# Order of one ScalarE copy and two exponentials in a multi-query attention kernel

## The chip, the cores and the metric

The kernel runs on one core of a Trainium2 chip. The metric is the device time of one execution in microseconds (us); smaller is better. The engines that matter here are TensorE (PE in the profile, with PEld for its weight loads), VectorE (DVE), ScalarE (ACT), GpSimd (POOL) and the DMA queue of SyncE (SP). Each engine executes its own list of instructions in the order in which the program wrote them and waits for others by semaphores.

## The reference

Residual multi-query attention over 64 sequences of 128 tokens with 512 features, 16 heads of 64 and one shared key and value head:

```python
xn = layernorm(x, g_in)
q = (xn @ Wq).reshape(b, n, H, DH).transpose(0, 2, 1, 3) * scale
kv = xn @ Wkv                      # k, v, with one null key and value put ahead
...
sim = jnp.einsum('bhid,bjd->bhij', q, k) + bias
sim = jnp.where(causal_mask, neg, sim)
sim = jnp.where(mask_p[:, None, None, :], sim, neg)
attn = jax.nn.softmax(sim, axis=-1)
out = jnp.einsum('bhij,bjd->bhid', attn, v)
out = out.transpose(0, 2, 1, 3).reshape(b, n, INNER) @ Wo
return x + layernorm(out, g_out)
```

All data is 32-bit floating point.

## The kernel before

The 64 sequences are worked in 32 pairs. After a first part that fills the pipeline, a loop calls `turn(d)` and `body(d)` for d = 1 to 29; three pairs at the end have code of their own. Everything is written out by hand in program order, under a manual schedule: the order of the calls in `body` is the order on each engine, and the framework only puts in the semaphore waits.

One `body(d)` holds the work of several pairs at once. With a = 2d and b = 2d+1 it computes the softmax of sequences a and b; with p = 2d-2 the output projection of the pair before; with l = 2d-4 the output layer norm, residual and store of the pair before that; and, for the group of four sequences g = d//2 + 1, half of its query projection. The parity h = d % 2 says which half: `f0` is the first tile of 128 query features in this call, `f1` the second. In bodies with h = 0 GpSimd also prepares sums of tokens (`token_sum`, `token_sums_inner`).

The query projection multiplies 2 by 2 blocks with seven products in place of eight (the Strassen-Winograd scheme). `product(g, f, k, pool, tag)` (matmul at L539) computes product k as two matrix instructions, which the profile shows as four matmul passes of 256 columns, into a PSUM bank with the tag "a" or "c". Bank "a" collects products 1, 6, 7 and 4 of a tile, one on top of the other. After each of the first three, `keep` (L551) has ScalarE copy the running sum out of the bank to SBUF (`kp` after product 1, `ku` after 6 and 7), and the next product into that bank must wait for this copy, since it adds to what is being read. Bank "c" collects products 5 and 3. `q_out` adds a kept copy to a bank on VectorE (L560) or, for the last one, copies it on ScalarE (L557). Product 2 is itself replaced by seven smaller ones (`inner_product`, L605, tile `pl`), and the output projection is built in the same way (`out_product`, L892; its first bank "X" is copied by ScalarE at L906 to `kyp`).

`exps(b, hf, lo, hi)` (L707) computes the exponentials of heads lo to hi-1 of one half of the rows: one ACTIVATE per head, each followed by a short read of its accumulator. Then `rinv` (L725, VectorE) and `scale` (L729, GpSimd) divide by the sums. `pair_norm` (L950, ScalarE, `yn`) and `norm_apply` (L301, ScalarE) are normalisations; `norm_stats` ends in a power on GpSimd at L280.

The stretch of `body` around the change, for TensorE: product 1 of tile f0, one or two inner products, the eight passes of `out_product(p, 1)`, then products 6, 5 and 7 of f0, then `out_product(p, 2)` (`pyw`). For ScalarE: the copy `kp`, `pair_norm(l)`, four exponentials of b, the copy `kyp`, two exponentials of b (heads 4 and 5), the copy `ku` of product 6, `pair_norm(l + 1)`, two more exponentials (heads 6 and 7), the copy `ku` of product 7, two `norm_apply`, one exponential of a, and the copy `qT` of bank "a" after product 4. Body 1 differs a little: there is no pair l yet, so that ScalarE has no `pair_norm` there, and a whole product 2 stands in place of the inner ones.

Of the kernel before, what the change touches and what calls it, by code (L numbers as in the profile page):

```python
# [17 lines left out]
def kernel(  # L18
# [504 lines left out]
    def product(g, f, k, pool, tag, start=True):  # L523

        if start:
            prod[tag] = pool.tile([P, HT], FP, tag=tag, name=f"p{tag}_{g}_{f}_{k}")
        lo, hi = xT[g][:, 0 : GB // 2], xT[g][:, GB // 2 :]
        t1, t2, t3, t4 = (xS.get((g, i)) for i in range(1, 5))
        w, t = {
            1: (a11, lo[:, :, lo_k]),  # L530
            2: (a12, lo[:, :, hi_k]),
            3: (s4, hi[:, :, hi_k]),
            4: (a22, t4),
            5: (s1, t1),
            6: (s2, t2),
            7: (s3, t3),
        }[k]
        for kc in range(HK):
            nc.tensor.matmul(  # L539
                prod[tag],  # L540
                w[:, kc, f * P : (f + 1) * P],
                t[:, :, kc, :],
                start=(start and kc == 0),
                stop=(kc == HK - 1),
                skip_group_check=not start,
            )

    def keep(tag, name, slot=None):
        slot = slot or name
        kept[name] = bp.tile([P, HT], FP, tag=f"k{slot}", name=f"k{name}", bufs=1)  # L550
        nc.scalar.copy(kept[name], prod[tag])  # L551
# [150 lines left out]
    def exps(b, hf, lo=0, hi=R8):  # L702
        if hf == 0 and lo == 0:
            rsum[b] = small.tile([P, 2, R8], FP, tag="rsum", name=f"rsum_{b}")
        for k in range(lo, hi):
            row = S[b][:, k, WITH_NULL[hf]]
            nc.scalar.activation(  # L707
                row,
                row,
                AF.Exp,  # L710
                bias=nmax[b][:, hf, k : k + 1],
                accum_out=rsum[b][:, hf, k : k + 1],
            )
# [146 lines left out]
    def out_sum(p, k, eng=nc.gpsimd):  # L860

        h11, h12 = oT[p][:, 0], oT[p][:, 1]
        h21, h22 = oT[p + 1][:, 0], oT[p + 1][:, 1]
        if k == 0:
            yS[p] = bp.tile([P, HC, N], FP, tag="yS", name=f"yS_{p}", bufs=1)
        o, a, b, op = (
            (yS[p], h21, h22, ALU.add),
            (h11, yS[p], h11, ALU.subtract),
            (h21, h22, h11, ALU.subtract),
            (h12, h12, h11, ALU.subtract),  # L870
        )[k]
        eng.tensor_tensor(o, a, b, op)  # L872
# [73 lines left out]
    def pair_norm(b, odd=(None, None)):  # L946
        nmr, rstd = nmrs.pop(b)
        pool, tag = odd if b % 2 else (ps_s, "s")
        yn[b] = pool.tile([P, DIM], FP, tag=tag, name=f"yn_{b}")
        nc.scalar.activation(yn[b], ys[b], AF.Identity, bias=nmr, scale=rstd)  # L950
# [318 lines left out]
    def body(d):  # L1269

        a, b, p, l = 2 * d, 2 * d + 1, 2 * d - 2, 2 * d - 4
        g, h = d // 2 + 1, d % 2
        q, soft = g < NG, d > 0
# [62 lines left out]
        if out:  # L1336
# [1 line left out]
            out_keep("X", "yp1", "yp1")  # L1338
            out_sum(p, 1)
            out_sum(p, 2)  # L1340
        if soft:
            exps(b, 0, 4, 6)
        if q:
            product(g, f0, 6, ps_q, "a", start=False)
            keep("a", "u2")
        if ln:
            pair_norm(l + 1, (ps_y, "Y"))
        if q:
# [253 lines left out]
    for d in range(1, PAIRS - 2):  # L1602
        turn(d)
        body(d)
# [42 lines left out]
```

## Time and profile before

| | |
|---|---|
| median of 3 runs | 1039.6 us (1039.45 to 1039.65) |
| the profiled execution, its own time | 1039.67 us |
| span of that execution in the trace | 1037.9 us |
| TensorE matmul busy | 1024.5 us, 99% |
| TensorE weight loads busy | 903.0 us, 87% |
| VectorE, ScalarE, GpSimd busy | 76%, 65%, 72% |
| from product 6 of one body to that of the second after it, in the middle of the run | 63.34 us (482.12 to 545.46), so 31.67 us a body with its turn |

The span is what the trace covers; the time of the execution is 1.8 us longer. A row of a timeline holds the start in us from the span's start, the length in us, the engine, the source line, the operation, the output and inputs, the shapes, how many instructions were merged ("x4"), and in brackets the idle time of the engine just before, with what ended it. A merged row's length runs from the first start to the last end. Matmuls are pipelined: the next starts before the last has ended, so rows of one engine overlap, and a matmul's end is modelled, while its start is recorded.

### The profile page before, as it was taken

Reading aid. Unit: us, or ns where it says so; the run is one execution under the profiler, and the core shown is the slowest. Engines: PE = TensorE matmul, PEld = TensorE weight load, DVE = VectorE, ACT = ScalarE, POOL = GpSimd, SP = SyncE. Lnnn points to the kernel's source line nnn. Section 1 sums busy time; section 2 is a strip of 40 time slices with the busy share of each in tenths; the row PEclk is TensorE's granted clock in tenths of the full one; section 3 lists DMA queues with packets and bytes.
Section 4 is the critical chain, followed back from the end, with each engine's and each line's share of the span. In section 5 each row is a group of like instructions: output and inputs, shape, how many; then the busy total and the mean of one; then the engine's idle time right before and its main releaser. Section 6 shows DMA issues by size and latency. Waiting matters only on the chain.

```text
span 1037.9 us, 31399 instructions
## 1 busy us (share of the span) xinstructions
PE 1024.5 (99%) x12337; PEld 903.0 (87%) x12337; DVE 788.7 (76%) x1774; ACT 675.7 (65%) x2709; POOL 745.1 (72%) x579
## 2 busy tenths in 40 slices
PE   9999999999999999999999999999999999999997
PEld 8888888888888888888888888888888888888886
DVE  6867777877778877778777778777787777877697
ACT  4756667666577565676656776666766657856582
POOL 4997668686785857758677686766868678586676
PEclk9999999999999999999999999999999999999999
DMA  6514152231613315133151521415223151331211
GB/s 215 167 40 135 63 171 77 77 112 63 182 66 103 99 60 176 63 123 108 41 166 62 158 85 47 148 62 172 76 83 110 62 183 62 104 82 33 93 63 63
DMA packets 69228, 105.14 MB, mean 101 GB/s; under 512 B 9044, under 2 KB 33496, under 8 KB 67288
## 3 DMA queue, kind: packets, MB, share of 16 engines
q1 hardware_dynamic: 68784, 102.73, 31.7%
q8 instruction: 97, 1.59, 0.6%
q14 instruction: 51, 0.42, 0.1%
q10 hardware_dynamic: 296, 0.40, 0.1%
HBM read 67.45 MB, written 35.65 MB: 99 GB/s over the span
## 4 chain that ended last, share of the span: by engine, by line
PE 85%; ACT 6%; DVE 6%; issue 1%; POOL 1%; DMA 0%; POOLq 0%; DVEq 0%; ACTq 0%
PE pa L539 17%; PE pyX L892 15%; PE pyY L892 10%; PE pc L539 7%; PE po L805 7%; PE pkv L353 6%; PE pyw L892 5%; PE pl L605 4%; ACT s L707 3%; PE ps L676 3%; PE pq L474 3%; PE sc_X L676 2%; DVE st L269 2%; DVE nmax L698 2%; PE sc_Y L676 2%; PE py_s L892 1%
## 5 line engine op out<-in xcount | busy, mean ns | idle before, releaser
L707 ACT ACTIVATE s<-s,nmax 128x65 f32<-128x65 f32 (+1 forms) x1024 | 372.7, 368 | 62.5 <-DVE nmax L698 62.5
L729 POOL TENSOR_TENSOR s<-s,rinv 128x512 f32<-128x512 f32 (+1 forms) x132 | 190.7, 1447 | 166.3 <-DVE rinv L725 166.3
L641 POOL TENSOR_TENSOR s<-biasp,mneg 128x1552 f32<-128x1552 f32 (+1 forms) x65 | 205.9, 3170 | 51.2 <-DVE s L691 38.2
L707 ACT ACTIVATION_READ_ACCUMULATOR s<-s,nmax 128x1 f32 x1024 | 195.6, 191 | 0.0
L557 ACT COPY qT<-pa 128x256 f32<-128x256 f32 x59 | 22.0, 373 | 172.0 <-PE pa L539 172.0
L539 PE MATMUL pa<-xS,wq 128*128 128x256 f32 x472 | 123.7, 385 | 3.6 <-ACT ku L551 2.6
L698 DVE TENSOR_REDUCE nmax<-s 128x8 f32<-128x1032 f32 (+1 forms) x128 | 121.7, 951 | 0.1
L745 DVE STREAM_TRANSPOSE sb<-s 128x1536 f32<-128x1536 f32 (+1 forms) x68 | 113.6, 1673 | 2.0 <-POOL s L729 2.0
L892 PE MATMUL pyX<-wo,oT 128*128 128x256 f32 x464 | 109.7, 379 | 0.0
L892 PE MATMUL pyX<-wT,oT 128*128 128x256 f32 x464 | 109.7, 379 | 0.0
L539 PEld LDWEIGHTS pa<-xS,wq 128*128 128x128 f32 x472 | 85.1, 190 | 23.9 <-POOL rstd L280 7.0
L892 PEld LDWEIGHTS pyX<-wo,oT 128*128 128x128 f32 x464 | 86.0, 190 | 10.5
L892 PEld LDWEIGHTS pyX<-wT,oT 128*128 128x128 f32 x464 | 85.9, 190 | 10.7
L872 POOL TENSOR_TENSOR oT<-oT 128x512 f32<-128x512 f32 x64 | 80.5, 1277 | 4.3 <-PE pyw L892 2.0
L560 DVE TENSOR_TENSOR qT<-pc,ku 128x256 f32<-128x256 f32 x118 | 48.7, 413 | 45.9 <-PE pc L539 29.7
L805 PE MATMUL po<-sb,vr 32*64 32x128 f32 (+1 forms) x3840 | 81.5, 310 | 0.0
L805 PEld LDWEIGHTS po<-sb,vr 32*64 32x64 f32 x3840 | 71.3, 131 | 8.1 <-issue 5.7
L621 DVE TENSOR_TENSOR qT<-pl,kp 128x128 f32<-128x128 f32 x112 | 31.3, 279 | 57.9 <-PE pl L605 55.7
L824 ACT ACTIVATE oT<-po,nv 128x512 f32<-128x512 f32 (+1 forms) x127 | 73.8, 654 | 0.1
L280 POOL TENSOR_TENSOR rstd<-rstd,nhalf 128x1 f32<-128x1 f32 x64 | 35.2, 559 | 46.6 <-DVE rstd L279 44.2
L353 PE MATMUL pkv<-wkv,xT 128*128 128x128 f32 x512 | 65.2, 281 | 0.0
L353 PEld LDWEIGHTS pkv<-wkv,xT 128*128 128x128 f32 x512 | 59.6, 191 | 5.0 <-DVE s L691 4.8
(185 smaller groups left out, 2379.0 us busy)
## 6 DMA issues: line engine op xcount, KB each, us to landing
res<-in_x_dram SPq DMA_DIRECT2D x64, 256.0 KB, 2.9
x<-in_x_dram SPq DMA_DIRECT2D x63, 256.0 KB, 4.5
out_dram<-y SPq DMA_DIRECT2D x63, 256.0 KB, 2.0
xd<-xb SPq DMA_DIRECT2D x14, 1024.0 KB
xT<-xd SPq DMA_DIRECT2D x56, 256.0 KB, 6.0
vr<-vd SPq DMA_DIRECT2D x64, 128.0 KB, 2.7
kT<-kd SPq DMA_DIRECT2D x64, 64.0 KB, 2.1
wo<-in_L_cond_Wo_dram SPq DMA_DIRECT2D x1, 2048.0 KB, 13.4
```

The source lines that it names most:

```text
L353: nc.tensor.matmul(pkv, xT[g][:, t, kc, :], wkv[:, kc, :], start=(kc == 0), stop=(kc == KC - 1),)
L539: nc.tensor.matmul(prod[tag], w[:, kc, f * P : (f + 1) * P], t[:, :, kc, :], start=(start and kc == 0), stop=(kc == HK - 1), skip_group_ch ...
L641: nc.gpsimd.tensor_tensor(S[b][:, :, keys], biasp[:, :, keys], mneg[:, t, keys] .unsqueeze(1) .broadcast_to([P, R8, keys.stop - keys.start ...
L676: nc.tensor.matmul(home[r][u * DH : (u + 1) * DH, f, :], qT[g, f, t // 2][rows, t % 2, hf, u], kT[g][rows, 0 : nk // Q, t, :], start=True, ...
L698: nc.vector.tensor_reduce(nmax[b][:, hf], S[b][:, :, WITH_NULL[hf]], AX.X, ALU.max, negate=True)
L707: nc.scalar.activation(row, row, AF.Exp, bias=nmax[b][:, hf, k : k + 1], accum_out=rsum[b][:, hf, k : k + 1],)
L729: nc.gpsimd.tensor_tensor(sv, sv, rinvs[b, hf][:, lo:hi].unsqueeze(2).broadcast_to([P, hi - lo, sv.shape[2]]), ALU.mult,)
L745: nc.vector.transpose(sbs[b][:, :, lo:hi].rearrange("p j e q -> p e j q"), S[b][:, lo:hi, 1 : ROW - 1].rearrange("p e (j k) -> p e j k", k=Q),
L805: nc.tensor.matmul(po[s][rows, to : to + n], vr[g][quad, j, t, :], sb[quad, slots, r * NF : (r + 1) * NF, :], start=(turn == 0), stop=True ...
L824: nc.scalar.activation(to, src, AF.Identity, bias=nv2)
L872: eng.tensor_tensor(o, a, b, op)
L892: nc.tensor.matmul(prod[key], h[:, c, :], w[:, c, :], start=(start and c == 0), stop=(c == HC - 1), skip_group_check=not start,)
```

## The change

The call of `exps(b, 0, 4, 6)` moves behind product 6 and its `keep`. On ScalarE the copy of bank "a" after product 6 then stands ahead of the exponentials of heads 4 and 5, not behind them. It happens once in each of the 29 bodies. The order on TensorE, VectorE, GpSimd and the DMA queue is the same as before; nothing is added or left out.

```diff
         if out:
             out_product(p, 1, ps_y, "X")
             out_keep("X", "yp1", "yp1")
             out_sum(p, 1)
             out_sum(p, 2)
-        if soft:
-            exps(b, 0, 4, 6)
         if q:
             product(g, f0, 6, ps_q, "a", start=False)
             keep("a", "u2")
+        if soft:
+            exps(b, 0, 4, 6)
         if ln:
             pair_norm(l + 1, (ps_y, "Y"))
         if q:
             product(g, f0, 5, ps_q, "c")
         if soft:
             exps(b, 0, 6)
             rinv(b, 0)
         if q:
             product(g, f0, 7, ps_q, "a", start=False)
             keep("a", "u3")
```

## The prediction

> **What bounds the kernel now.** I read the page first: busy shares, then the chain that ended last.
>
> ```profile
> span 1037.9 us, 31399 instructions
> ...
> PE 1024.5 (99%) x12337; PEld 903.0 (87%) x12337; DVE 788.7 (76%) x1774; ACT 675.7 (65%) x2709; POOL 745.1 (72%) x579
> ...
> PE 85%; ACT 6%; DVE 6%; issue 1%; POOL 1%; DMA 0%; POOLq 0%; DVEq 0%; ACTq 0%
> ```
>
> TensorE is busy for 99% and carries 85% of the chain. No other engine is above 76%. So only time in which TensorE stands still, or runs slower than its own pitch, can be won. Yet 6% of the chain runs through ScalarE, so somewhere TensorE waits for it. The groups by line say where:
>
> ```profile
> L539 PE MATMUL pa<-xS,wq 128*128 128x256 f32 x472 | 123.7, 385 | 3.6 <-ACT ku L551 2.6
> L539 PEld LDWEIGHTS pa<-xS,wq 128*128 128x128 f32 x472 | 85.1, 190 | 23.9 <-POOL rstd L280 7.0 <-ACT ku L551 6.9 <-POOL yS L872 0.5
> ```
>
> The matmuls into bank "a" with a weight from wq idled 3.6 us in all, 2.6 of them for a copy `ku`. Their weight loads idled longer: 6.9 us for `ku` and 7.5 for something on GpSimd. Next I read TensorE's timeline in one body with h = 0 (from 482) and one with h = 1 (from 514):
>
> ```profile
> 482.12 1.03 PE L539 MATMUL pa<-xS,wS 128*128 128x256 f32 x4
> 482.98 1.03 PE L539 MATMUL pc<-xS,wS 128*128 128x256 f32 x4
> 484.17 1.10 PE L539 MATMUL pa<-xS,wq 128*128 128x256 f32 x4 [0.17 <-ACT ku L551]
> 485.11 1.89 PE L892 MATMUL pyw<-wo,oT 128*128 128x256 f32 x8
> ...
> 487.50 1.03 PE L539 MATMUL pa<-xS,wq 128*128 128x256 f32 x4
> ...
> 514.68 1.03 PE L539 MATMUL pc<-xS,wS 128*128 128x256 f32 x4
> 515.78 1.13 PE L539 MATMUL pa<-xS,wq 128*128 128x256 f32 x4
> 516.75 1.89 PE L892 MATMUL pyw<-wo,oT 128*128 128x256 f32 x8
> ```
>
> These are products 6, 5 and 7, then `pyw`. A product takes 0.86 (482.12 to 482.98). Product 7 should start 0.86 after product 5, at 483.84; it starts at 484.17. The starts of the weight loads show the same:
>
> ```profile
> 482.76 0.84 PEld L539 LDWEIGHTS pc<-xS,wS 128*128 128x128 f32 x4
> 484.14 0.73 PEld L539 LDWEIGHTS pa<-xS,wq 128*128 128x128 f32 x4 [0.54 <-POOL rstd L280]
> ...
> 515.78 0.73 PEld L539 LDWEIGHTS pa<-xS,wq 128*128 128x128 f32 x4 [0.47 <-ACT ku L551]
> ```
>
> And ScalarE over the same body:
>
> ```profile
> 482.74 0.36 ACT L906 COPY kyp<-pyX 128x256 f32<-128x256 f32 x1
> 482.99 0.36 ACT L707 ACTIVATE s<-s,nmax 128x65 f32<-128x65 f32 x1
> ...
> 483.33 0.35 ACT L707 ACTIVATE s<-s,nmax 128x65 f32<-128x65 f32 x1
> ...
> 483.67 0.36 ACT L551 COPY ku<-pa 128x256 f32<-128x256 f32 x1
> 483.92 0.79 ACT L950 ACTIVATE yn<-y,nmro,rstdo 128x512 f32<-128x512 f32 x1
> ...
> 485.31 0.37 ACT L551 COPY ku<-pa 128x256 f32<-128x256 f32 x1
> ...
> 487.00 0.39 ACT L707 ACTIVATE s<-s,nmax 128x129 f32<-128x129 f32 x1
> ...
> 488.57 0.37 ACT L557 COPY qT<-pa 128x256 f32<-128x256 f32 x1 [1.08 <-PE pa L539]
> ```
>
> Product 6 ends at 482.12 + 1.03 = 483.15, but its copy starts only at 483.67, behind two exponentials; it ends at 484.03, and the weight load of product 7 starts at 484.14. The view blames a GpSimd power; that is the same wait, misnamed, since the matmul's own row names `ku` and those powers were over at 482.52 + 1.07 = 483.59:
>
> ```profile
> 482.52 1.07 POOL L280 TENSOR_TENSOR rstd<-rstd,nhalf 128x1 f32<-128x1 f32 x2
> ```
>
> **The change, part by part.** Nothing is added or removed; three ScalarE steps of each of 29 bodies change places. First, what the wait costs now. Body 1, which has no `pair_norm` and so an earlier ScalarE, does not stall, and gives the pitch:
>
> ```profile
> 71.25 1.03 PE L539 MATMUL pa<-xS,wS 128*128 128x256 f32 x4
> 72.11 1.03 PE L539 MATMUL pc<-xS,wS 128*128 128x256 f32 x4
> 72.97 1.03 PE L539 MATMUL pa<-xS,wq 128*128 128x256 f32 x4
> 73.84 1.89 PE L892 MATMUL pyw<-wo,oT 128*128 128x256 f32 x8
> ```
> ```profile
> 72.86 0.74 PEld L539 LDWEIGHTS pa<-xS,wq 128*128 128x128 f32 x4
> ```
>
> From the start of product 5 to that of `pyw` it takes 73.84 - 72.11 = 1.73. With h = 0 it takes 485.11 - 482.98 = 2.13, with h = 1 516.75 - 514.68 = 2.07. So a body loses 0.40 or 0.34. There are 14 bodies of each kind after body 1; one of the second kind, late already at its first copy, loses more:
>
> ```profile
> 641.37 1.03 PE L539 MATMUL pc<-xS,wS 128*128 128x256 f32 x4
> 642.75 1.13 PE L539 MATMUL pa<-xS,wq 128*128 128x256 f32 x4 [0.35 <-ACT ku L551]
> 643.72 0.59 PE L892 MATMUL pyw<-wo,oT 128*128 128x256 f32 x2
> ```
>
> 643.72 - 641.37 = 2.35, a loss of 0.62. The sum now: 14 x 0.40 + 13 x 0.34 + 0.62 = 10.6 us. The weight loads agree: 7.0 + 6.9 + 0.5 = 14.4 us idle over 28 stalls, 0.51 each. In step, a load would come 0.86 after that of product 5, at 483.62, which is 0.64 after product 5's own start. Body 1 shows that 72.86 - 72.11 = 0.75 still costs nothing; the load of 484.14 comes 1.16 after it, 0.41 too late.
>
> Second, when the copy comes in its new place. ScalarE is free for it at 482.99. The bank is ready when product 6 ends, 483.15, plus the release. In this position the release is not in the trace; the nearest row is the copy after product 1, into the same bank and with ScalarE idle:
>
> ```profile
> 542.64 1.03 PE L539 MATMUL pa<-xT,wq 128*128 128x256 f32 x4
> ```
> ```profile
> 543.77 0.37 ACT L551 COPY kp<-pa 128x256 f32<-128x256 f32 x1 [0.43 <-PE pa L539]
> ```
>
> 543.77 - 543.67 = 0.10. The copy after product 4 gives the lower end: 488.57 - (487.50 + 1.03) = 0.04. I take 0.10, the same instruction and the same kind of wait: the copy runs from 483.25 to 483.62. The lag from its end to the weight load is 484.14 - 484.03 = 0.11 with h = 0, so the load comes at 483.73, 0.75 after product 5: exactly what cost nothing in body 1. With h = 1 the lag is smaller:
>
> ```profile
> 515.37 0.36 ACT L551 COPY ku<-pa 128x256 f32<-128x256 f32 x1
> ```
>
> 515.78 - 515.73 = 0.05, which leaves 0.06 to spare. So the stall goes whole in all 28 bodies. If the release took 0.05 longer, only the 14 bodies with h = 0 would pay, 0.7 us.
>
> Third, what ScalarE pays. The copy now waits 483.25 - 482.99 = 0.26, and behind it in the queue wait the two exponentials (0.51 later: the wait and the copy's slot of 0.25), then `pair_norm(l + 1)`, the last two exponentials, the copy of product 7 and the two `norm_apply`, all 0.26 later. The copy of product 7 moves from 485.31 to 485.57 while its matmuls end earlier, so it is ScalarE that sets it. The cover is the idle 1.08 ahead of the copy `qT` at 488.57: product 4 comes 0.40 earlier, that copy is due at 488.17, and ScalarE, free at 487.00 + 0.39 + 0.26 = 487.65, still waits 0.5. From there on it is back in step with TensorE. Without that cover the 0.26 would go into the next copies, at most 28 x 0.26 = 7.3 us. VectorE takes from the late ones:
>
> ```profile
> 486.13 0.19 DVE L725 RECIPROCAL rinv<-rsum 128x8 f32<-128x8 f32 x1
> 486.25 0.37 DVE L560 TENSOR_TENSOR qT<-pc,ku 128x256 f32<-128x256 f32 x1
> ...
> 520.02 0.68 DVE L956 TENSOR_TENSOR y<-yn,res 128x512 f32<-128x512 f32 x1
> 521.07 0.42 DVE L560 TENSOR_TENSOR qT<-pc,ku 128x256 f32<-128x256 f32 x1 [0.38 <-PE pc L539]
> ```
>
> It gets to the add with the second `ku` at 486.25, when that copy, 485.57 + 0.37 = 485.94, is done; nothing slips. The thinnest place is in the body with h = 1: product 3, 0.34 earlier, would free VectorE's add at 520.73, and VectorE is done with the rows before it at about 520.70. It just keeps up; what it lost there would fall into its idle time behind.
>
> The sum against the profiled execution: span 1037.9 - 10.6 = 1027.3; around the span lie 1039.67 - 1037.9 = 1.8, so 1029.1. That execution is 0.07 above the median of the runs, so I say 1029.0.
>
> **Where a page bears on it.** The rows of "idle before" price the wait on the matmuls at 2.6 us, not 10.6. The Trainium skill, "Perfetto Trace Analysis", section "Per-engine timelines", says that the end of a TensorE instruction is estimated by the profiler from its size while its start is reported; by that rule the idle before a matmul is no measure, and starts are. This trace agrees: 0.17 idle where the next start is 0.40 late. Against the change speaks the Trainium skill, "PSUM — Partial Sum Buffer", section "Engine vs sequencer instructions", which calls ScalarE's queue strict first-in-first-out: what stands behind the waiting copy waits too, as reckoned above; `kp` at 543.77 shows such a wait.
>
> **The rivals.**
> - Part of the stall stays, or VectorE at 520.70 begins to hold product 5 of the next tile: a remainder of 0.05 to 0.15 a body, 1.4 to 4.2 us, time 1030.4 to 1033.2. For it: the margins of 0.00 and 0.03. Against: what is late falls into idle time of VectorE and ScalarE.
> - Only the matmul's idle rows come back, 2.6 us: 1037.0. Against: body 1, where the pitch is 1.73 with the copy early.
> - No effect, because something else holds product 7 at the same time, with h = 0 the GpSimd power by the view's name for it: then only h = 1 gains, 13 x 0.34 + 0.62 = 5.0 us, 1034.6; if both kinds are held, 1039.6. Against: the power ended 0.55 before.
> - Slower: the release of product 6 is not 0.10 but comes only with the end of product 5, right behind it (482.98 + 1.03 + 0.10 = 484.11). The copy would then start 0.44 later than today's 483.67, and product 7 with it: 28 x 0.44 = 12.3 us, 1051.9. It decides from a release of 0.52 on, where the new copy starts at 483.67. Against: `kp` started 0.10 after its product while TensorE went on with other products.
>
> **How the numbers follow.** Forecast 1029.0: 0.74. Partial: 0.11. GpSimd with h = 0: 0.04. Idle rows only: 0.03. No effect: 0.03. Slower: 0.05. A measurement tells about 0.2% from no change, 2.1 us; all cases but the last two are beyond it: faster 0.92, same 0.03, slower 0.05. The range goes from 1028.0 (another us, if small waits go along) to 1032.5, most of the partial case.
>
> **What would show it.** In the profile after: the weight load of product 7 at most 0.75 after product 5; product 5 to `pyw` 1.73 in every body; `ku` starting 1.13 after product 6 with about 0.26 idle before it; `qT` with about 0.5 idle; the step from body to body 31.67 - 0.37 = 31.30. The forecast is wrong if `ku` starts later than 1.20 after product 6, or if a new wait of TensorE appears behind it.

## The result, and the profile after

The changed kernel takes 1028.91 us (median of 5 runs, 1028.83 to 1029.29), the kernel before, run beside it, 1039.45 us (1039.26 to 1039.65). The ratio is 0.9899 with a 95% interval of 0.9885 to 0.9914. The forecast was 1029.0. The page of the profile after, its span, its busy shares and its chain of waits:

```profile
span 1027.1 us, 31399 instructions
...
PE 1017.6 (99%) x12337; PEld 904.7 (88%) x12337; DVE 787.5 (77%) x1774; ACT 677.5 (66%) x2709; POOL 745.4 (73%) x579
...
PE 97%; DVE 1%; POOL 1%; issue 0%; DMA 0%; POOLq 0%; DVEq 0%
```

The other engines and the weight loads are as busy as they were within 0.3%. TensorE's busy time fell by 6.9 us with the same instructions: most of the lost time had been counted as busy, as in the row of product 7 before, which showed 0.17 idle where 0.40 was lost. The chain shows the change best: ScalarE had 6% of it and is gone from it, TensorE has 97%. The groups by line, the same two as before:

```profile
L539 PE MATMUL pa<-xS,wq 128*128 128x256 f32 x472 | 121.2, 379 | 0.0
L539 PEld LDWEIGHTS pa<-xS,wq 128*128 128x128 f32 x472 | 86.4, 190 | 11.9 <-issue 0.2
```

The idle time for `ku` is gone, and so are the 7.5 us of the weight loads that the view before put down to GpSimd, though nothing on GpSimd was changed. Next TensorE's timeline after: product 6 of body 1, then products 6, 5, 7 and `pyw` of a body with h = 0, then product 6 of the same kind of body two later, and that of the last body:

```profile
70.92 1.03 PE L539 MATMUL pa<-xS,wS 128*128 128x256 f32 x4
...
477.35 1.03 PE L539 MATMUL pa<-xS,wS 128*128 128x256 f32 x4
478.22 1.03 PE L539 MATMUL pc<-xS,wS 128*128 128x256 f32 x4
479.08 1.03 PE L539 MATMUL pa<-xS,wq 128*128 128x256 f32 x4
479.94 1.89 PE L892 MATMUL pyw<-wo,oT 128*128 128x256 f32 x8
...
539.95 1.03 PE L539 MATMUL pa<-xS,wS 128*128 128x256 f32 x4
...
946.87 1.03 PE L539 MATMUL pa<-xS,wS 128*128 128x256 f32 x4
```

From product 5 to `pyw` it is 479.94 - 478.22 = 1.72, the pitch without a stall (2.13 before); in all 29 bodies it is 1.72 or 1.73. The weight load of product 7 in the same body:

```profile
478.96 0.75 PEld L539 LDWEIGHTS pa<-xS,wq 128*128 128x128 f32 x4
```

It comes 478.96 - 478.22 = 0.74 after product 5, within the 0.75 that cost nothing in body 1; with h = 1 it is about 0.68. The step from body to body is (539.95 - 477.35) / 2 = 31.30. From product 6 of body 1 to that of the last body it is 946.87 - 70.92 = 875.95 us. The row of the kernel before is:

```profile
957.49 1.03 PE L539 MATMUL pa<-xS,wS 128*128 128x256 f32 x4
```

957.49 - 71.25 = 886.24, so 10.29 us went between these points. The stall of the last body itself lies behind them: from product 5 to `pyw` it took 960.42 - 958.36 = 2.06 before and takes 949.46 - 947.73 = 1.73 now. With these 0.33 the change won 10.6 us. Another 0.33 is the start, 71.25 to 70.92, which no part of the change touches, and behind the last matmul (at 1030.14 before, 1019.18 after) the execution is 0.16 longer. Together that is the 10.8 us by which the span is shorter. And ScalarE's timeline after, in the body with h = 0:

```profile
477.98 0.35 ACT L906 COPY kyp<-pyX 128x256 f32<-128x256 f32 x1
478.47 0.37 ACT L551 COPY ku<-pa 128x256 f32<-128x256 f32 x1
478.74 0.35 ACT L707 ACTIVATE s<-s,nmax 128x65 f32<-128x65 f32 x1
...
480.79 0.35 ACT L551 COPY ku<-pa 128x256 f32<-128x256 f32 x1
...
482.46 0.39 ACT L707 ACTIVATE s<-s,nmax 128x129 f32<-128x129 f32 x1
482.76 0.19 ACT L707 ACTIVATION_READ_ACCUMULATOR s<-s,nmax 128x1 f32 x1
483.40 0.37 ACT L557 COPY qT<-pa 128x256 f32<-128x256 f32 x1 [0.45 <-PE pa L539]
```

The copy starts 478.47 - 477.35 = 1.12 after product 6, 0.09 after its modelled end, and the two exponentials follow. ScalarE is late for a while and meets TensorE again at `qT`, where by the view it now idles 0.45 (1.08 before).

### The profile page after: what moved, and what is told of

Same layout as the page of the kernel before. It is cut to its first block, busy times and chain, and to the rows that moved or that the text cites. A ratio compares the mean times of both kernels' runs of the same rounds, so it can differ in the third digit from the quotient of the medians.

```text
span 1027.1 us, 31399 instructions
## 1 busy us (share of the span) xinstructions
PE 1017.6 (99%) x12337; PEld 904.7 (88%) x12337; DVE 787.5 (77%) x1774; ACT 677.5 (66%) x2709; POOL 745.4 (73%) x579
## 4 chain that ended last, share of the span: by engine, by line
PE 97%; DVE 1%; POOL 1%; issue 0%; DMA 0%; POOLq 0%; DVEq 0%
PE pa L539 20%; PE pyX L892 20%; PE pyY L892 10%; PE pc L539 10%; PE po L805 7%; PE pkv L353 6%; PE pyw L892 5%; PE pl L605 4%; PE pq L474 3%; PE ps L676 3%; PE sc_X L676 2%; PE sc_Y L676 2%; PE py_s L892 1%; PE sc_a L676 1%; PE sc_w L676 1%
## 5 line engine op out<-in xcount | busy, mean ns | idle before, releaser
L539 PE MATMUL pa<-xS,wq 128*128 128x256 f32 x472 | 121.2, 379 | 0.0
L892 PEld LDWEIGHTS pyX<-wT,oT 128*128 128x128 f32 x464 | 85.9, 190 | 10.6
L621 DVE TENSOR_TENSOR qT<-pl,kp 128x128 f32<-128x128 f32 x112 | 31.0, 277 | 55.6 <-PE pl L605 53.8
L551 ACT COPY ku<-pa 128x256 f32<-128x256 f32 x118 | 43.4, 368 | 32.7 <-PE pa L539 24.4
```

The costliest lines, as they stand in the source:

```text
L539: nc.tensor.matmul(prod[tag], w[:, kc, f * P : (f + 1) * P], t[:, :, kc, :], start=(start and kc == 0), stop=(kc == HK - 1), skip_group_ch ...
L892: nc.tensor.matmul(prod[key], h[:, c, :], w[:, c, :], start=(start and c == 0), stop=(c == HC - 1), skip_group_check=not start,)
```

## The experiments

Seven kernels were run, each against the kernel before on the same chip; its median was 1039.77 us on both chips that were used. All of them change only the order of calls. The edits are shown against the changed kernel in the first, fourth, fifth and sixth experiment, against the kernel before in the others.

**One exponential back ahead of the copy.**

```diff
+        if soft:
+            exps(b, 0, 4, 5)
         if q:
             product(g, f0, 6, ps_q, "a", start=False)
             keep("a", "u2")
         if soft:
-            exps(b, 0, 4, 6)
+            exps(b, 0, 5, 6)
```

> One exponential goes back ahead of the copy of product 6, in all 29 bodies. Theory (the end of the copy sets the weight load of product 7, and a load at most 0.75 us after product 5 costs nothing): the copy starts 1.21 after product 6, its load comes 0.76 after product 5 with h = 1 and 0.82 with h = 0, so 14 bodies lose 0.07 and the others 0.01 at most: about 1 us over the changed kernel, 1029.9 us (1029.3 to 1030.5). Rival (each exponential ahead of the copy costs its own 0.335 slot): 28 x 0.335 / 2 = 4.7 us more or 1033.6 us. Rival (the order of the two exponentials against the copy matters as such): back to 1039.5 us.

Measured: 1030.21 us (1030.16 to 1030.35), ratio 0.9908 (0.9893 to 0.9922). TensorE's timeline, product 5 and `pyw`: with h = 0 (from 479), with h = 1 (from 510), and in body 19 (from 635):

```profile
479.04 1.03 PE L539 MATMUL pc<-xS,wS 128*128 128x256 f32 x4
...
480.83 1.89 PE L892 MATMUL pyw<-wo,oT 128*128 128x256 f32 x8
...
510.40 1.03 PE L539 MATMUL pc<-xS,wS 128*128 128x256 f32 x4
...
512.14 1.89 PE L892 MATMUL pyw<-wo,oT 128*128 128x256 f32 x8
...
635.75 1.03 PE L539 MATMUL pc<-xS,wS 128*128 128x256 f32 x4
...
637.76 1.46 PE L892 MATMUL pyw<-wo,oT 128*128 128x256 f32 x6
```

and the weight load of product 7 with h = 0:

```profile
479.86 0.73 PEld L539 LDWEIGHTS pa<-xS,wq 128*128 128x128 f32 x4 [0.20 <-POOL rstd L280]
```

The load comes 479.86 - 479.04 = 0.82 after product 5, and the body loses 480.83 - 479.04 - 1.73 = 0.06: late by 0.07 against the bound of 0.75, paid almost in full. With h = 1, where the load comes 511.17 - 510.40 = 0.77 after product 5, next to nothing is lost (512.14 - 510.40 = 1.74), but for body 19, which was the late one before too: 637.76 - 635.75 - 1.73 = 0.28. The sum is 14 x 0.06 + 0.28 = 1.1 us over the changed kernel; measured are 1.3. With h = 0 the copy starts 479.39 - 478.18 = 1.21 after product 6, 0.09 later than in the changed kernel. So of the 0.335 that an exponential takes, some 0.24 lies in the time in which ScalarE would wait for product 6 anyway, and both rivals fall. Here again the view names a GpSimd power for a load that moved with the copy alone.

**Three exponentials ahead of the copy.**

```diff
         if soft:
-            exps(b, 0, 4, 6)
+            exps(b, 0, 4, 7)
         if q:
             product(g, f0, 6, ps_q, "a", start=False)
             keep("a", "u2")
...
-            exps(b, 0, 6)
+            exps(b, 0, 7)
```

> Three exponentials (heads 4, 5 and 6) ahead of the copy, one more than in the kernel before. Theory: the copy ends one exponential, 0.335 us, later than before in every body, and nothing hides it any more: 28 x 0.335 = 9.4 us, and body 1, which had no stall, now loses about 0.34 too: 1039.5 + 9.7 = 1049.2 us (1048.5 to 1050). Product 5 to pyw: 2.46 with h = 0, 2.40 with h = 1. Rival (TensorE's stall comes from something beside the copy, the GpSimd power with h = 0): only 15 bodies lose, 1039.5 + 5.0 = 1044.5 us.

Measured: 1049.33 us (1049.12 to 1049.8), ratio 1.0092 (1.0077 to 1.0107). TensorE, products 5 and 7 and `pyw` with h = 0, then product 5 and `pyw` with h = 1:

```profile
103.43 1.03 PE L539 MATMUL pc<-xS,wS 128*128 128x256 f32 x4
104.95 1.10 PE L539 MATMUL pa<-xS,wq 128*128 128x256 f32 x4 [0.50 <-ACT ku L551]
105.89 1.46 PE L892 MATMUL pyw<-wo,oT 128*128 128x256 f32 x6
...
135.47 1.03 PE L539 MATMUL pc<-xS,wS 128*128 128x256 f32 x4
...
137.87 1.46 PE L892 MATMUL pyw<-wo,oT 128*128 128x256 f32 x6
```

105.89 - 103.43 = 2.46 with h = 0 and 137.87 - 135.47 = 2.40 with h = 1, both as expected and both 0.33 over the kernel before. So beyond the bound each us by which the copy is late is a us of TensorE, in both kinds of body.

**The new order only with h = 0.**

```diff
-        if soft:
+        if soft and h == 1:
             exps(b, 0, 4, 6)
         if q:
             product(g, f0, 6, ps_q, "a", start=False)
             keep("a", "u2")
+        if soft and h == 0:
+            exps(b, 0, 4, 6)
```

> The new order only in the 14 bodies with h = 0, the old one in those with h = 1. Theory (the view's name, the GpSimd power, is wrong and the copy holds both kinds of body): 14 x 0.40 = 5.6 us less than before, 1033.9 us (1033.3 to 1034.5), and the h = 1 bodies keep 2.07 from product 5 to pyw. Rival (with h = 0 the GpSimd power holds product 7): 1039.5 us.

Measured: 1034.1 us (1033.93 to 1034.67), ratio 0.9946 (0.9929 to 0.9962). TensorE, a body with h = 0 and the next with h = 1:

```profile
480.76 1.03 PE L539 MATMUL pc<-xS,wS 128*128 128x256 f32 x4
...
482.48 1.89 PE L892 MATMUL pyw<-wo,oT 128*128 128x256 f32 x8
...
512.06 1.03 PE L539 MATMUL pc<-xS,wS 128*128 128x256 f32 x4
...
514.12 1.89 PE L892 MATMUL pyw<-wo,oT 128*128 128x256 f32 x8
```

1.72 against 2.06: the changed bodies lose nothing, the others what they lost before. 1039.77 - 1034.1 = 5.7 us, against 14 x 0.40 = 5.6. That GpSimd caused the stall with h = 0 is excluded.

**The copy ahead of `kyp` too.**

```diff
         if out:
             out_product(p, 1, ps_y, "X")
-            out_keep("X", "yp1", "yp1")
-            out_sum(p, 1)
-            out_sum(p, 2)
         if q:
             product(g, f0, 6, ps_q, "a", start=False)
             keep("a", "u2")
+        if out:
+            out_keep("X", "yp1", "yp1")
+            out_sum(p, 1)
+            out_sum(p, 2)
```

> The copy of product 6 goes ahead of the copy of bank X (kyp) too, so that ScalarE is free for it 0.62 after product 6 starts, not 0.87. Theory (in the changed kernel the copy waits for the release of the bank, 0.10 after product 6 ends): it still starts 1.12 after product 6, ScalarE idles 0.5 ahead of it and only 0.2 ahead of the copy qT, and the time is that of the changed kernel, 1028.9 us within 0.5. Rival (the copy is started by ScalarE's own queue, and comes 0.25 earlier): weight load of product 7 earlier, the same time, but the copy 0.87 after product 6.

Measured: 1028.86 us (1028.77 to 1029.15), ratio 0.9895 (0.988 to 0.991), the time of the changed kernel. Product 6 and ScalarE around the copy, from the two timelines:

```profile
477.53 1.03 PE L539 MATMUL pa<-xS,wS 128*128 128x256 f32 x4
```
```profile
477.81 0.33 ACT L707 ACTIVATE s<-s,nmax 128x65 f32<-128x65 f32 x1
478.64 0.37 ACT L551 COPY ku<-pa 128x256 f32<-128x256 f32 x1 [0.40 <-PE pa L539]
478.91 0.38 ACT L906 COPY kyp<-pyX 128x256 f32<-128x256 f32 x1
```

The copy still starts 478.64 - 477.53 = 1.11 after product 6, with ScalarE idle 0.40 ahead of it. In the changed kernel it is the release of the bank by product 6, not ScalarE's queue, that sets the copy; nothing more is to be had by moving it further up. The idle time ahead of `qT` shrinks to 0.18, as expected.

**One more exponential in ScalarE's cover.** On the changed kernel, work is put ahead of the copy `qT`, where the prediction says that ScalarE's loss is hidden.

```diff
         if soft:
-            exps(a, 1, 0, 1)
+            exps(a, 1, 0, 2)
...
         if soft:
-            exps(a, 1, 1, 4)
+            exps(a, 1, 2, 4)
```

> The changed kernel, with one more exponential of a (129 columns, 0.385 us a slot) ahead of the copy qT of product 4, where the prediction says that the idle time hides what ScalarE lost. Theory: ScalarE idles 0.45 there, so one more fits: time as the changed kernel, 1028.9 us (within 0.6), idle ahead of qT about 0.06. Rival (there is no such cover): 28 x 0.385 = 10.8 us more, 1039.7 us.

Measured: 1029.23 us (1028.92 to 1029.53), ratio 0.9899 (0.9884 to 0.9914): the cover, idle time of ScalarE that hides its lateness, is there. The profiled execution was 0.6 us longer in its span than that of the changed kernel, and 0.74 us later already at product 6 of body 1 (71.66), ahead of all changed places; from there to product 6 of the last body (947.63) it took 875.97, against 875.95. In the body with h = 0 the last exponential ahead of `qT` starts at 483.60 and the copy at 484.16. With the 0.385 of an exponential between them, 0.17 of the cover is left, more than the 0.06 expected; the next experiment shows why.

**Two more.** As before, with `exps(a, 1, 0, 3)` ahead of the copy and `exps(a, 1, 3, 4)` behind.

```diff
         if soft:
-            exps(a, 1, 0, 1)
+            exps(a, 1, 0, 3)
...
         if soft:
-            exps(a, 1, 1, 4)
+            exps(a, 1, 3, 4)
```

> As e5, with two more exponentials (0.77 us) ahead of the copy qT. Theory: 0.77 - 0.45 = 0.32 is not covered; the copy ends at about 484.09 on the scale of the changed kernel's trace, where product 1 of the second tile, into the same bank, should start at 484.07 with its load by 483.96: load at 484.14, a loss of 0.18 to 0.20 a body, 28 bodies, 5.3 us: 1034.2 us (1032.5 to 1036). Rival (the cover is larger, ScalarE catches up later): 1028.9 us. Rival (the whole excess reaches TensorE): 28 x 0.32 = 9.0 us, 1037.9 us.

Measured: 1030.73 us (1030.69 to 1031.17), ratio 0.9915 (0.99 to 0.9929). The expected time was 1034.2, and 1030.73 lies below even the low end of its range, 1032.5: a miss, by the size of one term. TensorE's timeline, products 4 and 3, product 1 of the second tile and the matmul after it; then the weight load of that product 1; then ScalarE's last exponential ahead of the copy, and the copy:

```profile
483.34 1.03 PE L539 MATMUL pa<-xS,wq 128*128 128x256 f32 x4
484.20 1.03 PE L539 MATMUL pc<-xT,wS 128*128 128x256 f32 x4
485.06 1.09 PE L539 MATMUL pa<-xT,wq 128*128 128x256 f32 x4
485.99 0.38 PE L605 MATMUL pl<-xL,wq 128*128 128x128 f32 x2
```
```profile
485.02 0.73 PEld L539 LDWEIGHTS pa<-xT,wq 128*128 128x128 f32 x4 [0.20 <-ACT qT L557]
```
```profile
484.23 0.40 ACT L707 ACTIVATE s<-s,nmax 128x129 f32<-128x129 f32 x1
484.52 0.19 ACT L707 ACTIVATION_READ_ACCUMULATOR s<-s,nmax 128x1 f32 x1
484.62 0.36 ACT L557 COPY qT<-pa 128x256 f32<-128x256 f32 x1
```

The copy comes 484.62 - 483.34 = 1.28 after product 4, against 483.40 - 482.34 = 1.06 in the changed kernel, so it is late by 0.22 and not by 0.32. The cover was read off the idle time, 0.45, which the view counts from the end of the short accumulator read (482.76 + 0.19 = 482.95). But ScalarE takes its next instruction before that read is over: here the copy starts at 484.62, while the read ahead of it lasts to 484.52 + 0.19 = 484.71. An exponential's slot is 0.385 from start to start (484.23 to 484.62), so that in the changed kernel ScalarE was free at 482.46 + 0.385 = 482.85, 0.55 ahead of the copy. With 0.77 - 0.55 = 0.22 the rest follows: the load comes 0.82 after product 3 (485.02 - 484.20), 0.07 beyond the 0.75 that cost nothing, and the body loses 485.99 - 484.20 - 1.73 = 0.06: 28 x 0.06 = 1.7 us over the changed kernel; measured are 1.8. So the same bound holds at another product.

**Cover from TensorE instead.** ScalarE as in the kernel before; three inner products between products 5 and 7.

```diff
         if q:
             product(g, f0, 5, ps_q, "c")
+        if deep:
+            for k in (6, 5, 2):
+                inner_product(g, h, k)
...
         if deep:
-            for k in (6, 5, 2):
-                inner_product(g, h, k)
             inner_out(g, h, 0, 1, 0, "p1")
```

> ScalarE in the order of the kernel before; on TensorE the inner products 6, 5 and 2 (0.67 us) go between products 5 and 7, in the bodies from 2 on. Theory (the stall is nothing but product 7 coming too early for the copy): product 7 is due 0.67 later and no longer waits for the copy, in either kind of body. The inner products come earlier and may have to wait for VectorE's add out of bank pl: it ends 0.23 before their load with h = 0 (no loss), and 0.2 to 0.3 after it with h = 1. So 5.6 us are won with h = 0, and with h = 1 0.34 is swapped for about 0.30: 1039.5 - 6.4 = 1033.1 us (1032 to 1034.5). Rival (the gain comes from the exponentials or from ScalarE's order, not from product 7's wait): 1039.5 us.

Measured: 1033.09 us (1032.76 to 1033.79), ratio 0.9939 (0.9922 to 0.9955). TensorE with h = 0, product 5, the inner products and product 7, then with h = 1:

```profile
480.13 1.03 PE L539 MATMUL pc<-xS,wS 128*128 128x256 f32 x4
481.00 0.61 PE L605 MATMUL pl<-xL,wL 128*128 128x128 f32 x4
...
481.67 1.03 PE L539 MATMUL pa<-xS,wq 128*128 128x256 f32 x4
...
511.44 1.03 PE L539 MATMUL pc<-xS,wS 128*128 128x256 f32 x4
512.48 0.71 PE L605 MATMUL pl<-xL,wL 128*128 128x128 f32 x4
...
513.25 1.03 PE L539 MATMUL pa<-xS,wq 128*128 128x256 f32 x4
```

With h = 0 the stall is gone without any exponential moved: 481.67 - 480.13 = 1.54, product 5 and the inner products back to back. With h = 1 it is 1.81, 0.27 more, and the wait is another, as reckoned: the weight load of `pl` waits for VectorE's add at L621:

```profile
512.48 0.52 PEld L605 LDWEIGHTS pl<-xL,wL 128*128 128x128 f32 x4 [0.42 <-DVE qT L621]
```

So the gain is product 7's wait for the copy, whichever side gives way; but TensorE's order has a wait of its own behind it, and the change on ScalarE is the better one by 4.2 us.

## Why the prediction was right

- **What the stall cost.** 10.6 us by starts of matmuls; measured are 10.29 from product 6 of body 1 to that of body 29 and 0.33 in body 29 itself. The idle rows, 2.6 us, would have been wrong by a factor of four.
- **When the copy comes.** Predicted 1.13 after product 6, measured 1.12, with ScalarE free for it 0.24 earlier; the fourth experiment shows that the release of the bank sets it.
- **That no part of the stall stays.** With h = 0 the margin was put at 0.00, and this was the step most open to a miss. The load came at 0.74, not 0.75, and product 5 to `pyw` is 1.72. The first and second experiments show the bound from the other side: 0.82 after product 5 costs 0.06, three exponentials ahead cost 0.73. So the reckoning held, but with 0.01 or 0.02 to spare: the copy of the first experiment, 0.09 later, already cost 14 x 0.06 = 0.8 us in these bodies.
- **The misnamed releaser.** Argued from the end of the power in the prediction, shown by the third experiment. The likely reason why the view names GpSimd with h = 0 alone can be read in the kernel: in those bodies GpSimd makes the sum of tokens that product 7 reads (L521). In the trace before that sum runs from 481.30 to 482.57 and is done 1.57 ahead of the load.
- **What ScalarE and VectorE pay.** The second `ku` starts 480.79 - 477.35 = 3.44 after product 6 (3.45 predicted). The cover ahead of `qT` was put at 488.17 - 487.65 = 0.52, counted from the end of the exponential itself; the fifth and sixth experiments bound it between 0.385 and 0.77 and put it at 0.55. The miss of the sixth came from taking the view's 0.45 instead. VectorE just keeps up with h = 1, as its timeline after shows:

```profile
514.85 0.68 DVE L956 TENSOR_TENSOR y<-yn,res 128x512 f32<-128x512 f32 x1
515.57 0.42 DVE L560 TENSOR_TENSOR qT<-pc,ku 128x256 f32<-128x256 f32 x1
```

The add that idled 0.38 for product 3 before no longer idles, and TensorE does not wait for it. Whether a further gain of TensorE there would run into VectorE was not tried.

The span shrank by 0.2 more than forecast: 0.33 at the start less 0.16 behind the last matmul. The changed calls come after that start, and in the nine traces it varies from 70.92 to 71.66, so the 0.2 is not put down to the change.

## What to carry to other kernels

When an engine that sets the time waits for a copy out of a bank that it will write again, look at what stands ahead of that copy in the other engine's queue: work that nobody awaits soon can go behind it, if the engine meets a wait of its own later that covers the delay. Price such a stall by the starts of the bound engine's instructions against a stretch of the same code that does not stall; that stretch also shows a lateness that is still free. And measure the cover from the engine's slot, start to start, not from the end of a short row such as the accumulator read.

## What was not expected

- The weight load of a product may come 0.11 us later than in step (0.75 and not 0.64 after the start of the product before) at no cost, and 0.76 to 0.77 cost at most 0.01 in the first experiment; beyond that all of it is paid, 0.06 at 0.82, 0.40 at 1.16.
- The lag from the end of the copy to the weight load was 0.11 us with h = 0, where by the code product 7 needs a result of GpSimd made in the same body besides the copy, and 0.05 with h = 1, where it needs only the copy; the kernel before paid this 0.06 in 14 bodies. That the second engine makes the difference was not tested.
- Body 19 starts its first copy (`kp`) 0.28 us late, before the change, after it and in all experiments but the fourth, where it is in step with the other bodies. What delays it stays open.
